# Context products of two token tiles issued as one group, at two places per block instead of four

## The chip, the cores and the metric

The kernel runs on one core of one Trainium2 chip. The metric is the device time of one execution in microseconds; the time of a kernel is the median over its runs.

## The reference

The input is `x` of shape 128 x 64 x 768 (128 graphs with 64 tokens each) and an adjacency matrix of 64 x 64 per graph, all in fp32. Two layers follow each other, each with a residual and a layer norm without parameters. Cut to what matters:

```python
# layer 0, per graph
p = softmax(h @ h.T / sqrt(768));  delta = p * adj
attn = delta / (sum(delta) + 1e-10)
ctx = upper(attn) @ (h @ Wl.T + bl) + diag(attn) * (h @ Ws.T + bs) + lower(attn) @ (h @ Wr.T + br)
o = relu(layernorm(ctx) * gamma + beta)
x = layernorm(x + o)
# layer 1, per graph, 12 heads of 64
q, k, v = x @ Wq + bq, x @ Wk + bk, x @ Wv + bv
probs = softmax(where(adj > 0, q @ k.T / 8 + beta * adj, -9e15))
x = layernorm(x + probs @ v)
```

The line with `ctx` is what this change is about: for every token a row of attention weights times the "left" and "right" features of its graph, plus a diagonal weight times the "self" features.

## The kernel before

**Tiling.** 8192 tokens are cut into 16 blocks (`NBLK`) of 512 tokens, each of four token tiles (`T = 4`) of 128 tokens, that is of two graphs. The big projections (768 x 768 weights) are made as seven products in place of eight (a Strassen-like scheme): `seven` runs over `ORDER = (1, 2, 6, 5, 7, 4, 3)`, and for each of the seven over two halves of the tokens, so a projection has 14 products. They are numbered 0 to 13 here; each is a chain of three matmuls, and a 128 x 384 fp32 matmul shows as two instructions in the trace, so a product of the values projection is six instructions. After a product its PSUM bank is read by VectorE (`first` and `last`); products of the seven accumulate onto banks that VectorE must have read: product 6 and 7 open new `ps_Y` banks, and product 10 adds onto the `ps_X` bank of product 8, product 11 onto that of product 9.

**Order.** Layer 0 of block m = n + 1 and layer 1 of block n are interleaved by hand. `hooks` is a dictionary from a place in a projection to functions that are called just ahead of the product of that number; `val` holds the hooks of the values projection of block n (`values`), `qk` those of the query and key projections after it, `own`, `left` and `right` those of layer 0. From the loop over the blocks on, every engine executes its instructions in the order in which they are written. After each product `step` takes at most one piece of deferred work from queues (`first`, `urgent`, `lazy`); most of it is for VectorE, such as the transposes `turn0` puts there (six of them, for the tokens of block n + 2) or the weight sums of `deepened` in blocks 0 and 1.

**The context.** `context0(m)` returns one function per token tile, `part(t)`. It takes two PSUM banks from `ps_mm` (four in all, shared with scores, transposes and weighted sums), and makes four matmuls: for each half `h` of the 768 columns, and for each of the two graphs `g` of the tile, 64 columns of attention weights `aT` as the stationary operand against 384 columns of `lr` (left and right features stacked to 128 rows). The graph `g` decides which 64 of the 128 PSUM partitions the result goes to. Then VectorE does `o = o * dg + ps_ctx` for each half (L684), and for m > 0 ScalarE sums the finished tile (L687). `squares`, hooked in at place 9, begins with a VectorE instruction (L694) that needs the sums of all four tiles.

In every block but the last, the four parts are hooks of the values projection, `part(t)` at place `1 + 2 * t`:

```python
for t, f in enumerate(tiles):
    at(val, 1 + 2 * t, f)
```

For block 0 the four parts run one after another in the prologue, outside of any projection.

Of the kernel before, what the change touches and what calls it, by code (L numbers as in the profile page):

```python
# [11 lines left out]
F32 = mybir.dt.float32  # L12
AF = mybir.ActivationFunctionType
ALU = mybir.AluOpType
# [3 lines left out]
P = 128  # L18
B, L, D = 128, 64, 768
# [3 lines left out]
HALF = D // 2  # L23
# [28 lines left out]
def gnn_two_layers(ctx: ExitStack, tc, x, adj, wl, bl, ws, bs, wr, br, gamma, beta,  # L52
                   wq, bq, wk, bk, wv, bv, abeta, out):
    nc = tc.nc
# [14 lines left out]
    ps_mm = ctx.enter_context(tc.tile_pool(name="ps_mm", bufs=4, space=PSUM))  # L69
# [88 lines left out]
    def freed():  # L158

        while first:  # L160
            first.popleft()[1]()

    def settle(key):

        for queue in (first, urgent, lazy):
            while any(item[0] == key or item[0][0] == key for item in queue):
                queue.popleft()[1]()
# [6 lines left out]
    start = ExitStack()  # L174
# [489 lines left out]
    def context0(n):  # L664


        blk = blocks[n]
        xa, o, dg = blk["xa"], blk["x"], blk["dg"]
        by_act = n > 0
        if by_act:  # L670
            total, nm, var, std, rstd = (st.tile([P, T], F32, tag=f"c{k}", name=f"c{k}") for k in range(5))

        def unused():
            return l1s_p.tile([P, T * 4 * L], F32, tag="s", name="unused")[:, 0:D]

        def part(t):
            freed()
            for h in range(2):
                cols = slice(h * HALF, (h + 1) * HALF)
                ps = ps_mm.tile([P, 512], F32, tag="mm", name="ps_ctx")  # L680
                for g in range(2):
                    nc.tensor.matmul(ps[g * L : (g + 1) * L, 0:HALF], lhsT=blk["aT"][:, t, g * L : (g + 1) * L],  # L682
                                     rhs=blk["lr"][t][:, g, cols], start=True, stop=True)
                nc.vector.scalar_tensor_tensor(o[t][:, cols], o[t][:, cols], dg[:, t : t + 1], ps[:, 0:HALF],  # L684
                                               ALU.mult, ALU.add)
            if by_act:
                nc.scalar.activation(unused(), o[t], AF.Identity, accum_out=total[:, t : t + 1])  # L687
            elif t == T - 1:
                rest(moments(key, o, 1e-12))

        key = ("o", n)

        def squares():
            nc.vector.tensor_scalar(nm, total, -1.0 / D, None, ALU.mult)  # L694
            for t in range(T):
                nc.scalar.activation(unused(), o[t], AF.Square, bias=nm[:, t : t + 1], accum_out=var[:, t : t + 1])

        def roots():
            nc.vector.tensor_scalar(std, var, 1.0 / D, 1e-12, ALU.mult, ALU.add)
            nc.scalar.activation(std, std, AF.Sqrt)  # L700

        def inverse():
            nc.vector.reciprocal(rstd, std)
            rest([(nm[:, t : t + 1], rstd[:, t : t + 1]) for t in range(T)])

        def affine(t, mean, rstd):
            nc.vector.scalar_tensor_tensor(o[t], o[t], mean, affine_of["gamma"], ALU.add if by_act else ALU.subtract,
                                           ALU.mult)

        def affine2(t, mean, rstd):  # L710
            nc.vector.scalar_tensor_tensor(o[t], o[t], rstd, affine_of["beta"], ALU.mult, ALU.add)

        def residual(t):
            nc.vector.scalar_tensor_tensor(o[t], o[t], 0.0, xa[t], ALU.max, ALU.add)

        squared = 0 < n < NBLK - 1
        blk["x_d"] = x_d = tc.dram_tile([NTOK, D], F32, name=f"x1d_{n}") if squared else None

        def norm(t, mean, rstd):
            nc.vector.tensor_scalar(o[t], o[t], mean, rstd, ALU.subtract, ALU.mult)  # L720

        def stored():
            settle(key)
            for t in range(T):
                nc.gpsimd.dma_start(out=x_d[t * P : (t + 1) * P, :], in_=o[t])

        blk["stored"] = stored

        def rest(factors):
            for t, mr in enumerate(factors):  # L730
                fs = partial(affine, t, *mr), partial(affine2, t, *mr), partial(residual, t)
                later(key, *(fs if by_act else (fs[0], lambda fs=fs: (fs[1](), fs[2]()))))
            fs = [partial(norm, t, *mr) for t, mr in enumerate(moments(key, o, 1e-5))]
            later(key, *(fs if by_act else (lambda: (fs[0](), fs[1]()), lambda: (fs[2](), fs[3]()))))

        return [partial(part, t) for t in range(T)], (squares, roots, inverse)


# [283 lines left out]
    for n in range(NBLK):  # L1022
        m, p = n + 1, n - 1
        left, right, own, val = {}, {}, {}, {}
        qk = [{}, {}, {}]

        def at(hooks, place, f, *args):
            hooks.setdefault(place, []).append(partial(f, *args))
# [27 lines left out]
        if not last:  # L1056
            if n > 0:
                if m + 1 < NBLK:
                    at(left, 4, edges, m + 1)
                at(*((left, 11) if m < DEEP else (right, 13)), sides, m)  # L1060
                sq1 = {}

                def begin1():
                    blocks[n]["sq1"], sq1["fs"] = squares(blocks[n]["x_d"])


                when, place = (left, 10) if n > 1 else (right, 2)
                at(when, place, begin1)
                fetch = {}

                def begin2():
                    fetch["fs"] = loads(m)

                at(right, 8, begin2)
                for t in range(T):
                    at(right, 8 + t, lambda t=t: fetch["fs"][t]())
                for a in range(P // Q):
                    at(when, place + a, lambda a=a: sq1["fs"][a]())
                at(own, 0, settle, ("f", p))

                def turn1():
                    blocks[n]["xT"] = turned(("t1", n), blocks[n]["sq1"], f"xT_{n}")
                    later(("m", n), *mask(n), queue=urgent)

                at(own, 3, turn1)

                def sums1():
                    settle(("t1", n))
                    blocks[n]["S"] = combined(blocks[n]["xT"])

                at(own, 11, sums1)
                at(val, 0, lambda: combined4(blocks[n]["S"]))
                at(left, 6, lambda: combined4(blocks[m]["S"]))
                at(*((left, 4) if n > 1 else (right, 1)), blocks[n]["stored"])
                if m + 1 < NBLK:
                    sq = {}

                    def begin():
                        blocks[m + 1]["sq"], sq["fs"] = squares(x_b[m + 1])

                    at(own, 11, begin)
                    for a in range(P // Q):
                        at(own if a < 3 else val, 11 + a if a < 3 else 0, lambda a=a: sq["fs"][a]())
                if m == DEEP:
                    settle("d")
                if m < DEEP:
                    side_part(m, "l", None, left)
                    side_part(m, "r", None, right)
                    at(own, 0, lambda: nc.vector.tensor_tensor(bias_lr[:, :, HALF:D], bias_lr[:, :, HALF:D],
                                                               bias_lr[:, :, 0:HALF], ALU.subtract))  # L1110
                else:
                    for t, f in enumerate(both_sides(m, {**left, **{2 * len(ORDER) + k: f for k, f in right.items()}})):
                        at(own, 1 + t, f)
                self_part(m, None, own)
            tiles, normal = context0(m)
            for t, f in enumerate(tiles):
                at(val, 1 + 2 * t, f)
            for hooks, place, f in ((val, 9, normal[0]), (val, 13, normal[1]), (qk[0], 1, normal[2])):
                at(hooks, place, f)
            if m + 1 < NBLK:  # L1120

                def turn0():
                    blocks[m + 1]["hT"] = turned(("t", m + 1), blocks[m + 1]["sq"], f"hT_{m + 1}")

                at(val, 6, turn0)

                def scores0():
                    settle(("t", m + 1))
                    attention0(m + 1, False)

                def sums0():
                    blocks[m + 1]["S"] = combined(blocks[m + 1]["hT"], m + 1)

                at(qk[0], 4, scores0)
                at(qk[2], 8, sums0)
# [148 lines left out]
```

## Time and profile before

| what | value |
| --- | --- |
| time, median of 3 runs | 2917.6 us (2916.56 to 2920.24) |
| span of the profiled execution, first to last instruction | 2916.3 us |
| mean granted TensorE clock | 0.998 |
| TensorE matmul (PE) busy | 2872.5 us, 98% of the span |
| VectorE busy | 1974.3 us, 68% |
| ScalarE busy | 1122.4 us, 38% |
| one values projection with its four context parts, start of the first to start of the last matmul | 33.32 us |

The page gives the span of the profiled execution and no separate time for it; the span is 1.3 us below the median of the runs and 0.3 us below the fastest, so durations taken from it can be set against the run times without a correction. A values projection is run 16 times, 15 of them with the context parts of the next block inside.

In the timeline each row is a run of like instructions on one engine: start in us, length in us, engine, line, operation, names (out<-in), shape and count. A matmul's end is modelled and overlaps the next, so the distance between the starts of rows is what a piece takes.

### The profile page before, as it was taken

To read this page: it belongs to the slowest core of one execution; us is meant where nothing else is said; L and a number is where in the kernel's file an instruction comes from. 1 tells how busy PE (TensorE), PEld (TensorE's weight loads), DVE (VectorE), ACT (ScalarE), POOL (GpSimd) and SP (SyncE) were. 2 spreads that over 40 slices of the span, in tenths; PEclk is the share of its full clock that TensorE was granted. 3 is DMA by queue.
4 is the path that set the end of the run, shared out by engine and by line. 5 is a ranking of instruction groups with operands and counts; after the bars stand their busy time and mean duration, and the time that the engine had idled before them with its cause. 6 is when DMAs were issued, how large, how long until landed. Compare 5 with 4: busy or idle time off the path is not lost.

```text
span 2916.3 us, 49872 instructions
## 1 busy us (share of the span) xinstructions
PE 2872.5 (98%) x17578; PEld 1932.9 (66%) x17578; DVE 1974.3 (68%) x3973; ACT 1122.4 (38%) x2107; POOL 732.4 (25%) x879
## 2 busy tenths in 40 slices
PE   9999999999999999999999999999999999999997
PEld 5658567585665857658576675766757567585685
DVE  6678777676676766757667576766767667676655
ACT  0004224354243443434444344443434524344255
POOL 3133123213142140412405123051230512314110
PEclk9999999999999999999999999999999999999999
DMA  9788877859677595775958669486684956849443
GB/s 340 222 274 275 253 219 200 243 145 286 154 213 234 157 278 148 222 226 167 269 146 244 197 181 268 136 272 173 186 260 138 284 162 196 247 140 289 138 127 99
DMA packets 440662, 613.18 MB, mean 210 GB/s; under 512 B 53584, under 2 KB 416720, under 8 KB 440416
## 3 DMA queue, kind: packets, MB, share of 16 engines
q1 hardware_dynamic: 362960, 495.93, 56.1%
q10 hardware_dynamic: 60848, 44.05, 8.0%
q0 software_dynamic: 16608, 70.01, 6.7%
q8 instruction: 143, 2.34, 0.3%
q14 instruction: 103, 0.84, 0.1%
HBM read 539.43 MB, written 77.27 MB: 211 GB/s over the span
## 4 chain that ended last, share of the span: by engine, by line
PE 96%; POOL 2%; issue 1%; DVE 1%; ACT 0%; DMA 0%; POOLq 0%; SPq 0%; ACTq 0%
PE ps_X L389 38%; PE ps_Y L389 28%; PE ps_Y L643 11%; PE ps_X L643 10%; PE ps_ctx L682 3%; PE sc L833 2%; PE ps_y L884 2%; PE u L532 2%; POOL q L342 1%; POOL q L341 0%; PE ps_x L291 0%; POOL q L343 0%; ACT eT L853 0%; DMA xa<-in_x_dram 0%; DVE u_deep L443 0%
## 5 line engine op out<-in xcount | busy, mean ns | idle before, releaser
L389 PE MATMUL ps_X<-xT,wqk 128*128 128x256 f32 x1728 | 391.9, 380 | 0.6 <-ACT uqk L801 0.6
L853 ACT ACTIVATE eT<-s 32x256 f32<-32x256 f32 x768 | 317.8, 414 | 171.6 <-DVE s L862 161.6
L389 PEld LDWEIGHTS ps_X<-xT,wqk 128*128 128x128 f32 x1728 | 327.0, 190 | 52.9 <-ACT k L807 4.6
L322 POOL TENSOR_TENSOR S<-hT 128x768 f32<-128x768 f32 x16 | 29.0, 1810 | 1133.6 <-PE ps_Y L389 1102.1
L389 PE MATMUL ps_Y<-S,wqk 128*128 128x256 f32 x1152 | 264.3, 379 | 0.0
L687 ACT ACTIVATE unused<-o 128x768 f32<-128x768 f32 x60 | 50.6, 844 | 499.6 <-DVE o L684 305.3
L389 PEld LDWEIGHTS ps_Y<-S,wqk 128*128 128x128 f32 x1152 | 218.9, 190 | 29.8
L443 DVE TENSOR_TENSOR lr<-ps_Y,u_deep 128x384 f32<-128x384 f32 x273 | 151.6, 555 | 96.8 <-PE ps_Y L643 71.0
L643 PE MATMUL ps_Y<-wlr,q 128*128 128x384 f32 x546 | 208.5, 491 | 0.0
L801 ACT ACTIVATE uqk<-ps_X,bq 128x256 f32<-128x256 f32 x144 | 68.3, 474 | 333.1 <-PE ps_X L389 332.4
L389 PE MATMUL ps_X<-wv,xT 128*128 128x384 f32 x576 | 195.5, 489 | 0.0
L389 PE MATMUL ps_X<-ws,hT 128*128 128x384 f32 x540 | 179.2, 486 | 0.0
L809 DVE TENSOR_TENSOR q<-ps_Y,uqk 128x256 f32<-128x256 f32 x144 | 61.0, 424 | 169.7 <-PE ps_Y L389 97.4
L643 PE MATMUL ps_X<-wlr,q 128*128 128x384 f32 x364 | 152.0, 499 | 16.8 <-POOL q L342 5.9
L389 PEld LDWEIGHTS ps_X<-wv,xT 128*128 128x128 f32 x576 | 108.0, 190 | 80.4 <-issue 8.4
L894 DVE SCALAR_TENSOR_TENSOR o<-ps_y,rz,o 128x64 f32<-128x64 f32 x720 | 154.7, 277 | 6.4
L443 DVE TENSOR_TENSOR u_deep<-ps_X,lr 128x384 f32<-128x384 f32 x195 | 107.3, 551 | 68.3 <-PE ps_X L643 66.6
L389 PEld LDWEIGHTS ps_X<-ws,hT 128*128 128x128 f32 x540 | 102.5, 190 | 71.4
L643 PEld LDWEIGHTS ps_Y<-wlr,q 128*128 128x128 f32 x546 | 101.6, 190 | 67.2
L420 DVE TENSOR_TENSOR u<-ps_X,bv 128x384 f32<-128x384 f32 x96 | 53.4, 556 | 130.9 <-PE ps_X L389 130.9
L389 PE MATMUL ps_X<-S,wqk 128*128 128x256 f32 x576 | 138.3, 385 | 0.0
L389 PE MATMUL ps_Y<-xT,wqk 128*128 128x256 f32 x576 | 135.6, 385 | 0.0
(258 smaller groups left out, 5467.2 us busy)
## 6 DMA issues: line engine op xcount, KB each, us to landing
wlr<-lr_d SPq DMA_DIRECT2D x819, 192.0 KB, 3.4
wqk<-qk_d SPq DMA_DIRECT2D x672, 192.0 KB, 2.4
wv<-d_v SPq DMA_DIRECT2D x192, 192.0 KB, 2.9
ws<-d_s SPq DMA_DIRECT2D x180, 192.0 KB, 5.7
wv<-in_L_gnn_Wv_dram SPq DMA_DIRECT2D x144, 192.0 KB, 4.1
ws<-in_L_gnn_W_self_dram SPq DMA_DIRECT2D x135, 192.0 KB, 5.4
xa<-in_x_dram SPq DMA_DIRECT2D x64, 384.0 KB, 4.9
sq<-in_x_dram ACTq DMA_DIRECT2D x56, 384.0 KB, 7.8
```

Of the source, the lines that this page charges most:

```text
L389: nc.tensor.matmul(ps, lhsT=a, rhs=b, start=(c == 0 and i in (1, 2, 5)), stop=(c == len(fs) - 1), skip_group_check=True)
L420: recent["u"] = evicted[nm] = nc.vector.tensor_tensor(u, ps, bias[nm][:, b * HALF : (b + 1) * HALF], ALU.add)
L443: nc.vector.tensor_tensor(dst, view(ps), add, ALU.add)
L532: nc.tensor.matmul(u[g * L : (g + 1) * L, t, :], lhsT=xT[:, c, tok], rhs=xT[:, c, tok], start=(c == 0), stop=(c == KC - 1))
L643: nc.tensor.matmul(ps, lhsT=a, rhs=b, start=(k == 0 and j in (1, 2, 5)), stop=(k == len(fs) - 1), skip_group_check=True)
L682: nc.tensor.matmul(ps[g * L : (g + 1) * L, 0:HALF], lhsT=blk["aT"][:, t, g * L : (g + 1) * L], rhs=blk["lr"][t][:, g, cols], start=True, s ...
L801: nc.scalar.activation(u, ps, AF.Identity, bias=bias["qk"[j]][:, c : c + 1])
L809: nc.vector.tensor_tensor(dst, ps, part, ALU.add)
L833: nc.tensor.matmul(sc[r][g * L : (g + 1) * L, t, c, :], lhsT=q[rows, c, tok], rhs=k[rows, c, tok], start=True, stop=True)
L853: nc.scalar.activation(e[to[0], :, to[1]], pairs[rows, :, cols], AF.Exp)
L884: nc.tensor.matmul(y[r, h][cols, t, c, :], lhsT=eT[rows, 2 * h + t, c, cols], rhs=v[rows, 2 * h + t, g, hg + c * HC, :], start=True, stop= ...
L894: nc.vector.scalar_tensor_tensor(res[:, r, c, hg, :], ps[:, t, c, 0:HD], rz[:, t, c : c + 1], res[:, r, c, hg, :], ALU.mult, ALU.add)
```

## The change

The matmuls of two neighbouring tiles are issued together by a new function `multiplied`, which fills four banks of `ps_mm`; it is called from `part` of the even tiles. VectorE's and ScalarE's work stays in `part(t)`, per tile. The four parts are hooked in at places 1, 2, 5 and 6 instead of 1, 3, 5 and 7, so the matmuls of tiles 0 and 1 stand at place 1, those of tiles 2 and 3 at place 5, and the VectorE work of tiles 1 and 3 at places 2 and 6. `freed`, which empties the queue `first`, is called twice per block in place of four times. The number of matmuls, their shapes and their operands stay as they were.

```diff
+        banks = {}
+
+        def multiplied(ts):
+            freed()
+            for t in ts:
+                for h in range(2):
+                    ps = banks[t, h] = ps_mm.tile([P, 512], F32, tag="mm", name="ps_ctx")
+                    for g in range(2):
+                        nc.tensor.matmul(ps[g * L : (g + 1) * L, 0:HALF], lhsT=blk["aT"][:, t, g * L : (g + 1) * L],
+                                         rhs=blk["lr"][t][:, g, h * HALF : (h + 1) * HALF], start=True, stop=True)
+
         def part(t):
-            freed()
+            if t % 2 == 0:
+                multiplied((t, t + 1))
             for h in range(2):
                 cols = slice(h * HALF, (h + 1) * HALF)
-                ps = ps_mm.tile([P, 512], F32, tag="mm", name="ps_ctx")
-                for g in range(2):
-                    nc.tensor.matmul(ps[g * L : (g + 1) * L, 0:HALF], lhsT=blk["aT"][:, t, g * L : (g + 1) * L],
-                                     rhs=blk["lr"][t][:, g, cols], start=True, stop=True)
-                nc.vector.scalar_tensor_tensor(o[t][:, cols], o[t][:, cols], dg[:, t : t + 1], ps[:, 0:HALF],
-                                               ALU.mult, ALU.add)
+                nc.vector.scalar_tensor_tensor(o[t][:, cols], o[t][:, cols], dg[:, t : t + 1],
+                                               banks.pop((t, h))[:, 0:HALF], ALU.mult, ALU.add)
...
             tiles, normal = context0(m)
-            for t, f in enumerate(tiles):
-                at(val, 1 + 2 * t, f)
+            for place, f in zip((1, 2, 5, 6), tiles):
+                at(val, place, f)
```

## The prediction

> **What bounds the kernel now.** I read the page's busy shares first, then its chain that ended last:
>
> ```profile
> PE 2872.5 (98%) x17578; PEld 1932.9 (66%) x17578; DVE 1974.3 (68%) x3973; ACT 1122.4 (38%) x2107; POOL 732.4 (25%) x879
> ...
> PE 96%; POOL 2%; issue 1%; DVE 1%; ACT 0%; DMA 0%; POOLq 0%; SPq 0%; ACTq 0%
> ```
>
> TensorE is never idle for long, and 96% of the chain runs over it. Time is gained only by taking time from TensorE's own sequence, and lost only by making it wait. A busy share does not say whether TensorE streams at its pace, so I went to the timeline of TensorE over one values projection with the context parts inside (block 4; the 15 such stages agree to 3 ns):
>
> ```profile
> 915.46 2.10 PE L389 MATMUL ps_X<-wv,xT 128*128 128x384 f32 x6
> 917.49 1.51 PE L682 MATMUL ps_ctx<-lr,aT 128*64 128x384 f32 x8
> 918.93 2.20 PE L389 MATMUL ps_X<-wv,xT 128*128 128x384 f32 x6
> 920.97 2.10 PE L389 MATMUL ps_Y<-wv,xT 128*128 128x384 f32 x6
> 923.00 1.51 PE L682 MATMUL ps_ctx<-lr,aT 128*64 128x384 f32 x8
> 924.44 2.20 PE L389 MATMUL ps_Y<-wv,xT 128*128 128x384 f32 x6
> ...
> 937.49 7.90 PE L389 MATMUL ps_X<-wv,xT 128*128 128x384 f32 x24
> 945.23 4.03 PE L389 MATMUL ps_Y<-wv,S 128*128 128x384 f32 x12
> 949.10 2.11 PE L389 MATMUL ps_X<-xT,wqk 128*128 128x256 f32 x9
> ```
>
> Look at distances between starts. The undisturbed stretch 945.23 to 949.10 is 3.87 us for 12 matmuls: 0.3225 us each, 1.935 us for a product of six. A product ahead of a context part takes 917.49 - 915.46 = 2.03 us, one behind it 920.97 - 918.93 = 2.04 us. The context part itself takes 1.44 us; its instructions come in pairs, the two graphs side by side, so at the same pace four pairs would be 1.29 us. One insertion therefore costs 0.095 + 0.15 + 0.105 = 0.35 us beyond its work. The whole stage gives it more finely: 915.46 to 949.10 is 33.64 us; 14 products are 27.09, 16 pairs 5.16, and what is left, 1.39 us, is 0.348 us for each of four insertions. No wait row stands in it.
>
> Is that a price per insertion, or per token tile? The prologue answers, where the four tiles of block 0 stand together:
>
> ```profile
> 98.49 5.38 PE L682 MATMUL ps_ctx<-lr,aT 128*64 128x384 f32 x32
> 103.80 0.67 PE L291 MATMUL ps_x<-ident,rows 128*128 128x128 f32 x3
> ```
>
> 103.80 - 98.49 = 5.31 us for 16 pairs, 5.16 at the plain pace: 0.15 over, what the group of one tile shows as well. A tile boundary inside a group is free.
>
> **What the Trainium skill says.** "TensorEngine Tiling (Array Packing)", section "Key Properties": tiles work independently of each other, but changing the tiling mode, not just the tile, drains TensorE. The trace agrees on both: products use 128 columns (128*128), context matmuls 64 (128*64); graphs run side by side inside the group, and both edges cost. "TensorE: Matmul & The Clock Gate", section "Single matmul latency", puts the drain at about 175 ns for a bf16 matmul; two edges would be an estimated 0.35 us, and the trace has 0.348 in fp32. I use the trace's number. "Perfetto Trace Analysis", section "Tensor Engine Instruction (MATMUL, LD_WEIGHTS)", says a matmul's reported end is estimated; this trace shows rows overlapping, so I count starts only.
>
> **The change part by part.**
>
> *Matmuls.* None added or removed: 32 instructions (16 pairs) per block before and after. Two insertions of four go, in 15 blocks: 30 x 0.348 = **10.4 us**, all on TensorE's sequence, which is the chain. A stage goes from 33.64 to 32.94 us. Block 0's parts already stand together and gain nothing.
>
> *VectorE.* Eight context instructions per block stay; those of tile 1 move from ahead of the reading of product 3 to ahead of that of product 2, those of tile 3 from place 7 to 6. What TensorE could wait for is read off from VectorE's timeline:
>
> ```profile
> 917.59 0.56 DVE L420 TENSOR_TENSOR u<-ps_X,bv 128x384 f32<-128x384 f32 x1 [1.38 <-PE ps_X L389]
> 918.43 1.23 DVE L684 SCALAR_TENSOR_TENSOR o<-o,dg,ps_ctx 128x384 f32<-128x384 f32 x2 [0.28 <-PE ps_ctx L682]
> 921.17 0.56 DVE L420 TENSOR_TENSOR u<-ps_X,bv 128x384 f32<-128x384 f32 x1 [1.51 <-PE ps_X L389]
> 923.10 0.56 DVE L777 TENSOR_TENSOR v<-ps_Y,u 128x384 f32<-128x384 f32 x1 [1.38 <-PE ps_Y L389]
> ...
> 939.63 0.56 DVE L420 TENSOR_TENSOR u<-ps_X,bv 128x384 f32<-128x384 f32 x1 [2.42 <-PE ps_X L389]
> ```
>
> VectorE waits over a microsecond before most readings. I lay the new order on TensorE's starts, counted from the stage's start. The first group runs from 2.03 for 1.44 + 1.29 = 2.73 us, product 1 from 4.76, product 2 from 6.80, products 3 and 4 from 8.73 and 10.67, the second group from 12.70, products 5 to 8 from 15.43, 17.47, 19.40 and 21.34. VectorE reads product 1 at 7.00 (2.24 us after its start, as now), done 7.56; tile 1 takes 1.23 us, to about 8.8; product 2 can be read from 8.93. So nothing is late there, and product 2's reading, done at 9.5, is needed by product 6 at 17.47.
>
> *Banks.* The first group takes all four `ps_mm` banks. Tile 0's come free near 4.2, tile 1's, now held until VectorE has passed product 1, near 8.8. The second group wants them from 12.70: 3.9 us to spare. No other user of `ps_mm` stands in the values projection. This is the one wait that the change lengthens, and I price it at nothing, covered by products 2 to 4; without that cover each microsecond late is one microsecond of TensorE per block.
>
> *Second half.* Tile 3's instructions follow the reading of product 5 (done 18.23) and end at 19.5; two transposes of about 1.1 us end by 21.7. Product 8 is read at 23.48, done 24.03, and product 10 needs it at 25.21: 1.2 us to spare, as now. In blocks 0 and 1, two batches of weight sums (about 1.5 us each) stand there too: 18.23 + 1.5 + 1.2 + 1.5 = 22.5, still ahead of 23.48.
>
> *ScalarE and queues.* The four sums of 0.84 + 0.18 us stay; the last comes one place earlier, so the VectorE instruction at place 9 that needs it (L694) does not wait longer. Emptying `first` at places 3 and 7 goes; VectorE's timeline shows no work from it there. SP's, ScalarE's and POOL's DMA issues are not reordered among themselves; in the waits view TensorE waited for DMA twice, 7.1 us, both for `xa` at transposes outside these stages. Weights that must arrive 0.7 us earlier per block of some 179 us are a demand 0.4% denser; I take nothing, with 1 us either way as bound, and another 1 us for the prologue, whose order is not written out by hand.
>
> **Sum.** 2916.3 - 10.4 = 2905.9 us of span for the profiled execution. The median stands 1.3 us above that span, so 2917.6 - 10.4 = **2907.2 us**, 0.36% less. About 0.2%, 5.8 us, is what a measurement of this kernel can tell from no change.
>
> **Rivals.**
>
> *A new wait takes part of it.* VectorE's late reading or the held banks stall TensorE by 0.2 to 0.7 us per block, 3 to 10 us in all: 2910.2 to 2917.2. For it: only 0.1 us lies between tile 1's end and product 2's reading. Against: that reading is needed 8 us later.
>
> *The price belongs to the work, not the edge.* If a longer group paid anew at each tile, nothing would be gained: 2917.6. The prologue's group of 32 speaks against it.
>
> *Slower.* Product 8's reading slips behind tile 3's instructions, the transposes and the weight sums, and product 10 waits. VectorE must be more than 1.2 us late before anything is lost; a stall of 0.70 us per block eats the gain, and 1.1 us per block gives 15 x 1.1 - 10.4 = 6 us more: about 2924. It would take VectorE 2.3 us late in every block where the profile shows it idle for 2.42 us before that same reading.
>
> **How the numbers follow.** Forecast 0.86, own range 2904.5 to 2910 (10.4 us with 1 us each for DMA and prologue and about 1 us of spread in the runs); part of it 0.06, half of which still beats 0.2%; nothing gained 0.05; slower 0.03. Faster 0.89, within 0.2% 0.08, slower 0.03. The range 2904.5 to 2911 keeps the forecast and the near end of the first rival.
>
> **What would show it.** Right: TensorE's timeline with context rows of x16 lasting 2.73 us from start to start, two per values stage, product rows beside them still 2.03 and 2.04, and the stage at 32.94 us. The bank wait would show as a TensorE idle time before L682 that VectorE's context instruction ends, at place 5; the late reading as an idle time before a product at L389. Wrong: context rows over 2.8 us, or stages at 32.94 with the saved 0.7 us returned as waits in the projections behind.

## The result, and the profile after

| | before | changed |
| --- | --- | --- |
| median of 6 runs each | 2917.0 us | 2907.53 us |
| all runs | 2916.36 to 2920.24 us | 2906.74 to 2908.64 us |
| span of the profiled execution | 2916.3 us | 2905.9 us |
| values stage with context parts, from its first matmul's start to the start of the projection behind it | 33.64 us | 32.95 us |

The ratio is 0.9967, 95% interval 0.9955 to 0.9978: faster by 0.33%, and by more than 0.2% also at the near end of the interval. The forecast was 2907.2 us for the time, 2905.9 us for the span and 32.94 us for the stage.

TensorE's timeline of the changed kernel over the stage shown of before (rows as there; L684 is the line of the context matmuls now):

```profile
912.41 2.10 PE L389 MATMUL ps_X<-wv,xT 128*128 128x384 f32 x6
914.44 2.80 PE L684 MATMUL ps_ctx<-lr,aT 128*64 128x384 f32 x16
917.17 2.20 PE L389 MATMUL ps_X<-wv,xT 128*128 128x384 f32 x6
919.21 4.03 PE L389 MATMUL ps_Y<-wv,xT 128*128 128x384 f32 x12
923.08 2.10 PE L389 MATMUL ps_X<-wv,S 128*128 128x384 f32 x6
925.11 2.80 PE L684 MATMUL ps_ctx<-lr,aT 128*64 128x384 f32 x16
927.84 2.20 PE L389 MATMUL ps_X<-wv,S 128*128 128x384 f32 x6
...
945.36 2.75 PE L389 MATMUL ps_X<-xT,wqk 128*128 128x256 f32 x12
```

Read the starts again. A context group now holds 16 instructions and takes 917.17 - 914.44 = 2.73 us, twice the plain 1.29 plus one 0.15. The product ahead of it takes 2.03 us, the one behind 2.04 us, as before, but two products per stage pay each of these in place of four. Products 2 and 3 (919.21, x12), which a context part used to stand between, take 923.08 - 919.21 = 3.87 us, their plain 1.935 us each. The page's busy line moved little, since TensorE was and is busy nearly all the time:

```profile
PE 2862.8 (99%) x17578; PEld 1938.6 (67%) x17578; DVE 1968.4 (68%) x3973; ACT 1121.9 (39%) x2107; POOL 731.2 (25%) x879
```

The count of matmuls is the same, 17578; TensorE was busy 2872.5 us before and 2862.8 us now. A 9.7 us fall in "busy" time with no matmul removed is a reminder that a modelled row covers the edge as well as the work.

VectorE in the same stage:

```profile
915.38 1.23 DVE L692 SCALAR_TENSOR_TENSOR o<-o,dg,ps_ctx 128x384 f32<-128x384 f32 x2 [0.28 <-PE ps_ctx L684]
919.41 0.56 DVE L420 TENSOR_TENSOR u<-ps_X,bv 128x384 f32<-128x384 f32 x1 [2.80 <-PE ps_X L389]
919.88 1.13 DVE L692 SCALAR_TENSOR_TENSOR o<-o,dg,ps_ctx 128x384 f32<-128x384 f32 x2
921.34 0.56 DVE L785 TENSOR_TENSOR v<-ps_Y,u 128x384 f32<-128x384 f32 x1 [0.33 <-PE ps_Y L389]
...
935.88 0.56 DVE L420 TENSOR_TENSOR u<-ps_X,bv 128x384 f32<-128x384 f32 x1 [2.21 <-PE ps_X L389]
```

Tile 1's two instructions (919.88) carry no wait: their matmuls have long ended. They end at 921.01, 0.33 us before VectorE can read product 2. Before the reading of product 8 (935.88) VectorE still waits 2.21 us for TensorE.

### The profile page after: what moved, and what is told of

Same layout as the page of the kernel before. It is cut to its first block, busy times and chain, and to the rows that moved or that the text cites. A ratio compares the mean times of both kernels' runs of the same rounds, so it can differ in the third digit from the quotient of the medians.

```text
span 2905.9 us, 49900 instructions
## 1 busy us (share of the span) xinstructions
PE 2862.8 (99%) x17578; PEld 1938.6 (67%) x17578; DVE 1968.4 (68%) x3973; ACT 1121.9 (39%) x2107; POOL 731.2 (25%) x879
## 4 chain that ended last, share of the span: by engine, by line
PE 96%; POOL 2%; issue 1%; DVE 1%; ACT 0%; DMA 0%; POOLq 0%; SPq 0%; ACTq 0%
PE ps_X L389 38%; PE ps_Y L389 28%; PE ps_Y L643 11%; PE ps_X L643 10%; PE ps_ctx L684 3%; PE sc L841 2%; PE ps_y L892 2%; PE u L532 2%; POOL q L342 1%; POOL q L341 0%; PE ps_x L291 0%; POOL q L343 0%; ACT eT L861 0%; DVE u_deep L443 0%; DMA xa<-in_x_dram 0%
```

## The experiments

The theory is the prediction's: switching TensorE between 128 and 64 columns and back costs 0.348 us, whatever is done in between. Each run below is set against runs of the kernel before made beside it (medians 2917.05 to 2917.62 us). "Stage" in the table is the distance from the first to the last values matmul's start, one matmul (0.32 us) less than in the table above: 33.32 us before and 32.62 us in the changed kernel.

| run | insertions per block | time, us | ratio to before | stage, us |
| --- | --- | --- | --- | --- |
| single parts at the new places | 4 | 2917.41 | 1.000 (0.9991 to 1.0008) | 33.32 |
| groups, work at the old places | 2 | 2907.82 | 0.9965 (0.9952 to 0.9978) | 32.62 |
| full width | 4, without change of width | 2896.28 | 0.9927 (0.9911 to 0.9944) | 31.93 |
| one group | 1 | 2901.62 | 0.9945 (0.993 to 0.996) | 32.28 |
| halves | 8 | 2938.12 | 1.0072 (1.0057 to 1.0087) | 34.71 |
| beside u | 0 | 3071.55 | 1.0527 (1.0509 to 1.0544) | 26.77 |
| beside u, spread | 0 | 3143.61 | 1.0783 (1.0765 to 1.0801) | 26.77 |
| beside u, reload later | 0 | 3077.45 | 1.0548 (1.053 to 1.0565) | 26.77 |

In the last three the context has left the values stage, so their 26.77 us is the plain stage.

**Grouping or places?** The change does two things: it groups matmuls and it moves VectorE's work. Two runs do one each. First the kernel before with its parts at the new places:

```diff
-            for t, f in enumerate(tiles):
-                at(val, 1 + 2 * t, f)
+            for place, f in zip((1, 2, 5, 6), tiles):
+                at(val, place, f)
```

> The kernel before with its four separate context parts moved to places 1, 2, 5 and 6, nothing grouped. Theory (each insertion of 64-column matmuls among 128-column ones costs 0.348 us of TensorE): four insertions remain, so the stage stays at 33.32 us from its first to its last values matmul and the time at 2917 us. Rival (the places are what gained, because VectorE's work lies better): the stage falls to 32.62 us and the time to about 2907 us without any grouping.

Then the changed kernel with the old places:

```diff
-            for place, f in zip((1, 2, 5, 6), tiles):
+            for place, f in zip((1, 3, 5, 7), tiles):
```

> The changed kernel with VectorE's and ScalarE's work of tiles 1 and 3 back at places 3 and 7; the matmuls stay grouped at places 1 and 5. Theory: two insertions per block, stage 32.62 us, 2907 us; the banks of tile 1 are then held until product 2 has been read, near 10 us into the stage, still ahead of the second group's need at 12.7 us. Rival (places matter, or the held banks do): above 2910 us, with TensorE idle ahead of the second group until VectorE's context instruction ends.

The places alone did nothing and the grouping alone did all of it. In the first run a product between two insertions pays both of its edges (TensorE's timeline of that run):

```profile
917.73 1.51 PE L682 MATMUL ps_ctx<-lr,aT 128*64 128x384 f32 x8
919.17 2.20 PE L389 MATMUL ps_X<-wv,xT 128*128 128x384 f32 x6
921.30 1.51 PE L682 MATMUL ps_ctx<-lr,aT 128*64 128x384 f32 x8
```

921.30 - 919.17 = 2.13 us against 1.935: one product length of distance between two insertions shares nothing. In the second run VectorE ends with tile 1 at 921.70 + 1.13 = 922.83, and the second group starts at 924.99 without a wait, so the held banks have over 2 us to spare even with tile 1's work one place later than in the change.

**Is it the width?** An insertion could also cost through its weights, its banks or its waits. In this run the insertions stay, but not the width:

```diff
-                for g in range(2):
-                    nc.tensor.matmul(ps[g * L : (g + 1) * L, 0:HALF], lhsT=blk["aT"][:, t, g * L : (g + 1) * L],
-                                     rhs=blk["lr"][t][:, g, cols], start=True, stop=True)
+                nc.tensor.matmul(ps[:, 0:HALF], lhsT=blk["aT"][:, t, :], rhs=blk["lr"][t][:, 0, cols],
+                                 start=True, stop=True)
```

> The kernel before, four insertions at its old places, but each pair of 64-column matmuls is replaced by one 128-column matmul of the same length in columns streamed (384). This leaves out the second graph of each tile: all 128 rows are multiplied with the first graph's features. Theory (the price is the change of width, not the insertion): no price at all, 4 x 0.348 x 15 = 20.9 us gone, stage 31.93 us, 2896 us. Rival (an insertion costs its 0.35 us whatever its width, through its weights, its banks or its waits): 2917 us. Anything between splits the price.

The whole price went. TensorE's timeline of this run:

```profile
908.39 2.10 PE L389 MATMUL ps_X<-wv,xT 128*128 128x384 f32 x6
910.32 1.45 PE L681 MATMUL ps_ctx<-lr,aT 128*128 128x384 f32 x4
911.61 2.10 PE L389 MATMUL ps_X<-wv,xT 128*128 128x384 f32 x6
913.55 2.10 PE L389 MATMUL ps_Y<-wv,xT 128*128 128x384 f32 x6
```

910.32 - 908.39 = 1.93, 911.61 - 910.32 = 1.29, 913.55 - 911.61 = 1.94 us: the same banks, the same VectorE work and the same four places, at the plain pace. What differs is the shape, 128*128 for 128*64, and with it the number of instructions and weight loads (four per insertion for eight) and that graphs no longer run side by side on two halves of the columns. This run does not part these; a comparison under "No insertion at all" goes further.

**Per insertion, whatever its length?** Eight insertions of two pairs each:

```diff
-        def part(t):
+        def part(t, halves=(0, 1)):
             freed()
-            for h in range(2):
+            for h in halves:
...
-                at(val, 1 + 2 * t, f)
+                at(val, 1 + 2 * t, f, (0,))
+                at(val, 2 + 2 * t, f, (1,))
```

> The kernel before with each context part split into its two halves of 384 columns, eight insertions per block at places 1 to 8 of the values projection, two pairs of matmuls each. Theory: the price is per insertion whatever its length, so 4 x 0.348 x 15 = 20.9 us above before, 2938 us, stage 34.71 us. Rival (the price shrinks with a shorter group, because part of it hides behind the neighbours' weight loads): between 2917 and 2930 us.

And one insertion of sixteen pairs:

```diff
-            for place, f in zip((1, 2, 5, 6), tiles):
+            for place, f in zip((1, 1, 1, 2), tiles):
```

> The changed kernel with all four tiles' matmuls in one group at place 1, through the same four banks: the matmuls of tiles 2 and 3 go into the banks that VectorE has just read for tiles 0 and 1; tile 3's VectorE work stands at place 2. Theory: one insertion per block, 3 x 0.348 x 15 = 15.7 us below before, stage 32.28 us, 2901.3 us; the bank of tile 0 is read by 4.2 us and wanted again at 4.76, as in the prologue's group of 32, which shows no gap. Rival (four banks are too few, or the reading of product 1 comes too late behind eight context instructions): TensorE stalls inside the group or at product 5, 0.35 us or more per block, and the time is 2907 us or above.

Both came out as the theory has it. The stages from zero to eight insertions are 31.93 (full width), 32.28, 32.62, 33.32 and 34.71 us: 0.35 us for each insertion, whether it holds two pairs or sixteen. The one group is 6 us faster than the change itself and beats both kernels. Its four banks did not bind, apart from block 1, where VectorE enters the stage late, behind the mask's instructions, and the stage took 32.34 us. TensorE and VectorE in that run, each from its own timeline:

```profile
913.54 5.38 PE L684 MATMUL ps_ctx<-lr,aT 128*64 128x384 f32 x32
918.85 2.20 PE L389 MATMUL ps_X<-wv,xT 128*128 128x384 f32 x6
```

```profile
914.48 3.82 DVE L692 SCALAR_TENSOR_TENSOR o<-o,dg,ps_ctx 128x384 f32<-128x384 f32 x6 [0.27 <-PE ps_ctx L684]
```

5.31 us for 16 pairs is what the prologue showed: VectorE empties two banks in 1.2 to 1.3 us, TensorE fills two in 1.29.

**No insertion at all.** Next to matmuls that are 64 columns wide already, the context would have no edges of its own:

```diff
-            for place, f in zip((1, 2, 5, 6), tiles):
-                at(val, place, f)
-            for hooks, place, f in ((val, 9, normal[0]), (val, 13, normal[1]), (qk[0], 1, normal[2])):
+            for f in tiles:
+                at(qk[0], 4, f)
+            for hooks, place, f in ((qk[0], 8, normal[0]), (qk[0], 12, normal[1]), (qk[1], 1, normal[2])):
```

> All four context parts leave the values projection and stand directly ahead of the score products u of the next layer 0 at place 4 of the first query and key projection, which are 64 columns wide too; squares, roots and inverse move behind them to places 8 and 12 there and place 1 of the second. Theory: no insertion of its own is left in 14 blocks and one in the last, so 14 x 4 x 0.348 + 3 x 0.348 = 20.5 us below before, 2896.8 us, the values stage 26.8 us. Rival (the layer norm of layer 0 now begins some 16 us later and its VectorE work is flushed at once where the block is stored, or ScalarE's sums hold up the readings of the query and key products): waits of 0.3 us or more per block come back, in the query and key projections or in the left part of layer 0, and the time is 2901 us or above.

The values stage fell to its plain 26.77 us, and beside u the context paid no edge. That is seen best in the run after this one, which has the context at the same place without a wait inside it; here is TensorE's timeline of "beside u, spread", and then that of the kernel before, where u stands alone:

```profile
816.83 5.38 PE L684 MATMUL ps_ctx<-lr,aT 128*64 128x384 f32 x32
822.04 2.97 PE L532 MATMUL u<-hT 128*64 128x64 f32 x96
824.93 2.86 PE L389 MATMUL ps_X<-S,wqk 128*128 128x256 f32 x12
```

```profile
954.38 3.02 PE L532 MATMUL u<-hT 128*64 128x64 f32 x96
957.32 2.86 PE L389 MATMUL ps_X<-S,wqk 128*128 128x256 f32 x12
```

Context and u take 824.93 - 816.83 = 8.10 us, u alone 957.32 - 954.38 = 2.94 us. The difference, 5.16 us, is 16 pairs at the plain pace, with nothing on top. The same narrow matmuls, with their own weight loads and with two graphs side by side, thus cost 0.35 us more among 128-column matmuls and nothing more among 64-column ones: the price is that of the switch. Narrow and side by side go together in this kernel; which of the two makes it a switch stays open.

Everything else in the run went wrong. The waits view of TensorE in that run (who waited for whom, us in total, times, longest):

```profile
PE ps_X L389 <- ACT uqk L809: 53.8, 30, 3.6
PE ps_X L643 <- POOL q L342: 42.3, 25, 3.5
PE ps_ctx L684 <- DVE o L692: 24.1, 13, 1.9
```

All of TensorE's waits add up to 153 us there against 29 before. The first row is ScalarE: its four squares of block m, some 1.1 us each, stand ahead of its reading of a query product, and TensorE waits 3.1 us for it at 821.70. The second is the store of the block: its DMA issues wait on POOL's queue for VectorE's late layer norm, and the sums that TensorE needs stand behind them. The third is a bank wait inside the group. And some of the long waits cost more than themselves (stretches of that run: from and to, length, busy time and count of PE, PEld, DVE, ACT and POOL, granted TensorE clock, DMA share, GB/s):

```profile
815.82:821.70 5.88, 2.75 (x14) 2.09 (x12) 1.12 (x6) 4.52 (x10) 0.00 (x0) 0.91 0.46 129
821.70:826.98 5.28, 5.28 (x13) 4.20 (x14) 1.56 (x5) 0.79 (x2) 0.00 (x0) 0.50 0.15 37
439.80:450.00 10.20, 7.07 (x34) 6.22 (x34) 3.42 (x9) 6.04 (x13) 0.00 (x0) 1.00 0.36 103
```

After the wait that ends at 821.70 the granted clock is 0.50, and the twelve instructions of two query and key products, which take 2.6 us elsewhere in this run, take 5.28 us. The Trainium skill, "TensorE: Matmul & The Clock Gate", section "HAM oscillation — how this bites in real kernels", tells of idle gaps of TensorE above about 3.4 us that bring the clock down to half. Here a wait of 3.1 us was enough, and the clock fell before it was over: a mean of 0.91 over the 5.88 us that end with the wait is an estimated 1.1 us at 0.50. But the length of the wait does not settle it. The third row holds the same wait in an earlier block (3.13 us, to 442.95), with the clock at 1.00 all through. Of the 13 waits of 3.12 or 3.13 us at this place in the run, five left the clock alone, four were followed by some 3.4 us at half and four by some 6.8 us.

The run's mean clock is 0.981 against 0.998: 1.7% of 3076 us is 52 us, an estimate on the high side, since part of the slow time lies inside the waits. With 153 - 29 = 124 us of waits that makes up to 176 us, close to the 180 that lie between the measured span of 3075.8 us and the 2895.8 expected.

I then moved apart what had collided:

```diff
-            if by_act:
-                nc.scalar.activation(unused(), o[t], AF.Identity, accum_out=total[:, t : t + 1])
-            elif t == T - 1:
+            if not by_act and t == T - 1:
...
-                when, place = (left, 10) if n > 1 else (right, 2)
+                when, place = right, 2
...
-                at(*((left, 4) if n > 1 else (right, 1)), blocks[n]["stored"])
+                at(right, 1, blocks[n]["stored"])
...
-            for hooks, place, f in ((qk[0], 8, normal[0]), (qk[0], 12, normal[1]), (qk[1], 1, normal[2])):
+            for t in range(T):
+                at(qk[0], 6 + t // 2, blocks[m]["summed"], t)
+            at(qk[1], 4, lambda: blocks[n]["swaps"]())
+            for hooks, place, f in ((qk[0], 12, normal[0]), (qk[1], 6, normal[1]), (qk[1], 7, normal[2])):
```

(`summed` is the sum of a tile taken out of `part`, `swaps` ScalarE's swap of the values taken out of `values`.)

> As the run beside u, with what it collided with moved apart: ScalarE's four sums stand at places 6 and 7 of the first query and key projection, the squares at 12, roots and inverse at places 6 and 7 of the second, ScalarE's swap of the values (whose buffer is one of the context's features) begins at place 4 of the second, and the store of the block and its reload go to places 1 and 2 of the right part. Theory: the 155 us that the run beside u lost came from ScalarE's order, which made TensorE wait for its readings, from the store that held up POOL's queue, and from the slower clock after such waits; apart from them the edges are gained, and the time is near 2897 us. Rival (VectorE's layer norm work, begun 16 us later, does not fit before the block is stored wherever the store stands): TensorE waits stay, and the time is above the 2901.6 us of the one group.

That theory fell: slower still, 209 us of waits. The bank wait was gone and the store's wait smaller, but a new one stood on top, 102.8 us in all. It shows in one block (TensorE, VectorE, then ScalarE, each from its own timeline):

```profile
937.21 1.01 PE L643 MATMUL ps_X<-wlr,q 128*128 128x384 f32 x1 [8.69 <-DVE u_deep L443]
```

```profile
936.06 0.17 DVE L929 TENSOR_SCALAR f<-f 128x4 f32<-128x4 f32 x1 [10.18 <-ACT unused L955]
```

```profile
924.88 7.21 ACTq L301 DMA_DIRECT2D sq<-x1d  x2
932.20 0.84 ACT L955 ACTIVATE unused<-o 128x768 f32<-128x768 f32 x1 [20.04 <-DMA sq<-x1d]
```

The reload of the block just stored (`sq<-x1d`) is issued from ScalarE's queue, and ScalarE is held at it for 7.2 us; its sums for the last layer norm stand behind, VectorE behind those, and TensorE behind VectorE. So it was neither what I had named nor what the rival named, but a transfer. The next run moves it:

```diff
-                when, place = right, 2
+                when, place = right, 9
...
-            at(qk[1], 4, lambda: blocks[n]["swaps"]())
-            for hooks, place, f in ((qk[0], 12, normal[0]), (qk[1], 6, normal[1]), (qk[1], 7, normal[2])):
+            at(qk[1], 12, lambda: blocks[n]["swaps"]())
+            for hooks, place, f in ((qk[0], 12, normal[0]), (qk[1], 2, normal[1]), (qk[1], 3, normal[2])):
```

> As the spread run, with the reload of the stored block (issued on ScalarE's queue right behind the store) moved from places 2 to 5 of the right part to places 9 to 12, the roots to place 2 and the inverse to place 3 of the second query and key projection, and the swap of the values to its place 12. Theory: the wait of 8 to 9 us per block in the spread run was ScalarE holding the reload back until the store had landed, with the last layer norm's sums and VectorE queued behind it; it goes, with the slow clock after it, and the time falls by over 100 us, to 2900 to 3010 us. Rival (VectorE's layer norm work itself is late): the wait stays near 100 us in all and the time above 3050 us.

Half a hit: that wait fell from 102.8 to 2.8 us, but the time only by 66 us, to where the rival had put it. Two waits took its place, both in the self part (waits view of TensorE in this run):

```profile
PE ps_Y L389 <- DVE o L596: 49.6, 13, 6.5
PE ps_X L389 <- DVE u L420: 32.1, 23, 3.7
```

In one block (from 1114.22 us on) the reload holds ScalarE for 9.3 us again, now ahead of the output's last step, whose store then keeps the buffers of the next `o`: VectorE waits 9.2 us for that store and 5.1 us for the reload. So VectorE is late there because of transfers, not, as the rival had it, because its own work does not fit. Whether some order gains the last edges stays open; three orders lost 154 to 226 us looking for the 5 us between one insertion and none.

## Why the prediction was right

**The price per insertion.** 0.348 us was read off the stage of before. The stage changed from 33.321 to 32.624 us between its first and last matmul's start, 0.697 us for two insertions; 15 stages give 10.45 us, and the span fell by 10.4. The runs with 0, 1, 2, 4 and 8 insertions to pay for fit the same number; the full width run and the context beside u show that it hangs on the switch of width. What TensorE does in the 0.348 us, a drain or something else, no run shows: that the estimate of two drains came near it is no evidence, since that figure is for the latency of a bf16 matmul.

**A tile boundary inside a group is free.** Shown by 2.73 us for 16 instructions and 5.31 us for 32.

**VectorE.** Laid out were readings of product 1 at 7.00, product 2 at 8.93 and product 8 at 23.48 us into the stage; they came at 7.00, 8.93 and 23.47. Tile 1 ended at 8.60, 0.2 us ahead of the 8.8 put down: they began at 7.47, while the row of the reading still ran to 7.56, and took 1.13 us, where the rows that wait for a matmul take 1.23.

**Banks.** The second group started at 12.70 us, as laid out, without a wait. The lengthened hold cost nothing here, and nothing with tile 1's work one place later.

**The rest of the kernel.** TensorE's waits, 29.3 us in all before, are 28.6 us after; the saved time did not come back as waits in every block. In one block it did in part: at 1565.23 TensorE waits 0.81 us in the left part, where it waits 0.45 in the other blocks and in the kernel before, and 0.35 us of the gain is gone (what held it the trace does not name); the run with groups at the old places has the same wait. The first stage, on the other hand, starts at 194.93 us and not at 195.18, so the prologue gave 0.25 us. That the span fell by just what was forecast, to 0.1 us, is the luck that these two cancel; the 1 us allowed for the prologue covers its shift.

**The offset.** I put the median 1.3 us above the profiled span, from the page of before. For the changed kernel the profiled execution's own time is on hand: 2907.63 us for a span of 2905.9, and every other execution with both numbers has 1.7 us around its span too. The profiled execution of before, with 2916.3 us of span, then took an estimated 2918.0 us, 1 us more than the median of its six runs (2917.0). So the spans are 10.4 us apart and the medians 9.5. The forecast started from 2917.6, the median of the first three runs; from 2917.0 it would have been 2906.6. That it came within 0.3 us of the median is in part luck. The run times cannot tell 9.5 from 10.4 us, since their interval reaches from 6.4 to 13.1; the stages can.

**The rivals.** The wait that takes part of the gain showed in one block alone, with 0.35 us and not where that rival had put it, and the price that belongs to the work did not show. The one that ended slower needs VectorE over 1.2 us late; in this change it still waits 2.21 us for TensorE at that place. The runs beside u show that such lateness does happen in this kernel as soon as work of ScalarE and VectorE is moved by a projection and not by one product, and that it then costs more than the edge.

## What to carry to other kernels

Where TensorE is the bound, look at distances between the starts of rows on both sides of every change of matmul shape: here a switch from 128 to 64 columns and back cost 0.35 us, which no wait row and no busy share shows, and it was paid per visit and not per matmul (other widths and types were not tried). Gather narrow matmuls into as few visits as PSUM banks and their readers allow; here, with one engine filling two banks in the time another empties two, four banks carried a group of 32 instructions. Before moving a group to a place where the edge is free, count what else moves with it, on the other engines and on the queues that issue their transfers.

## What was not expected of the hardware

A wait of TensorE of 3.1 us was followed, at 821.70 in the run beside u, by 5.3 us at a granted clock of 0.50, so the wait cost about twice its length. The same wait at 442.95 left the clock at 1.00 and cost only itself, so what a long wait costs cannot be read off its length. In the kernel before, which keeps TensorE at 98%, the granted clock is 1.00 up to its last matmul, and the mean of 0.998 comes from the end of the span behind it; the slow clock appears under matmuls only in the runs that make TensorE wait for long.
